# A graph layer and an attention layer on one core: weights reloaded into a third buffer, a store behind a write, and row maxima moved forward

## The chip, the cores and the metric

The kernel runs on one core of one Trainium2 chip. The metric is the device time of one execution in microseconds (us). Engines: TensorE (PE, with its weight loads PEld), VectorE (DVE), ScalarE (ACT), GpSimd (POOL), and SyncE (SP), which issues every DMA of this kernel from one queue.

## What is computed

128 graphs of 128 nodes with 512 features, float32. Layer 0 is a graph convolution, layer 1 attention with 8 heads of 64; both take a layer norm with a relu, and both are added to x. The reference, cut:

```python
h = jnp.maximum(_layernorm(x, axis=-1), 0.0)
norm_adj = adj * deg_inv_sqrt[:, None] * deg_inv_sqrt[None, :]
x = x + jnp.einsum('nm,bmo->bno', norm_adj, jnp.einsum('bni,io->bno', h, weight)) + bias
h = jnp.maximum(_layernorm(x, axis=-1), 0.0)
q, k, v = (h @ Wq + bq), (h @ Wk + bk), (h @ Wv + bv)          # split into 8 heads
scores = jnp.einsum('bqhd,bkhd->bhqk', q, k) / jnp.sqrt(64)
scores = scores + (1.0 - adj)[None, None, :, :] * -1000000000.0
out = jnp.einsum('bhqk,bkhd->bqhd', jax.nn.softmax(scores, axis=-1), v)
x = x + out @ Wo + bo
```

## The kernel before

**Groups and blocks.** The batch is cut into 32 groups of 4 elements, a group into two halves of 2. The loop over t (line 1252) runs up to five blocks per round: W (graph layer's weight product for group t + 1), Q, K and V (projections of group t) and Y (attention's output product of group t - 1). Scores of group t and attention of group t - 1 stand at V0. Each block is one product of 512 x 512 x 512 by the 2 x 2 scheme of Strassen and Winograd with seven products, and inside it by a second such level; a block has seven steps, 0 to 6. Combinations of operands are additions on POOL (line 94 and lines 411 to 414), and the sums out of PSUM are additions on DVE (L478 and L493).

**PSUM.** Six banks have names: a0, a1, d0, d1, b, c. Bank c holds the seventh product, in three pieces (PHASES, line 70): piece 0 in step 6 of its own block, pieces 1 and 2 put off into steps 1 and 2 of the next block through the list `tail` (lines 557, 567, 575 and 624). Piece 2 adds to a quarter that the reads of piece 1 take, so it follows those reads. In block Y these are pieces of v's product: `bank_c<-w,op_h` on TensorE, `v<-v,bank_c` on DVE.

**The order of the work.** Nothing is scheduled by a planner: the order is written by hand. `at(t, place, f, ...)` puts a call into a plan; the place names a block, a step and a part ("V3b" is block V, step 3, ahead of the step's second part; c comes after it). `block` (line 1150) issues what is planned for a place, then that part of the step. Engines run their own instructions in the order of issue, and tiles carry the waits between engines.

**Softmax.** Scores are written to `att` (L872 on DVE with the mask for elements 0, 1 and 2; for element 3 ACT copies, L869, and POOL adds the mask later, `add_mask`, L880, planned at V4). `row_max` (L884) takes the maxima on DVE, ACT the exponentials (L896), POOL the scaling (L907). Then `flip_att` (L914) transposes 32 x 32 blocks on DVE and writes them to DRAM (L915, named `turned<-att`), and `turn_att` (L786, `att<-turned`, four DMAs) reads them back turned. `attend` (L940) multiplies by v in the order 2, 3, 0, 1.

**Weights.** Two of three buffers `w_buf` alternate between q, k, v and o; the third holds the graph layer's weights. A buffer is reloaded by `reload_w` (line 1116, DMA at L1127) in five parts of 8 slots, 512 KB each, at places that `reloads_of` gives; a reload waits until TensorE has read the old weights there. In t = 1 the weights with all their combinations are written once to DRAM by `keep_w` (L211); o's stand until then in the buffer op_o, which attention fills at V0.

**DMA.** SP's queue is one: an issue that waits (a turn for its write, a reload for a buffer) holds all behind it. `store_half` (L958) writes 512 KB of output.

Of the kernel before, what the change touches and what calls it, by code (L numbers as in the profile page):

```python
# [8 lines left out]
F32 = mybir.dt.float32  # L9
# [39 lines left out]
SLOTS = 40  # L49


PARTS = ((0, 8), (8, 16), (16, 24), (24, 32), (32, 40))
# [45 lines left out]
def kernel(  # L98
# [18 lines left out]
    P = 128  # L117
# [4 lines left out]
    NG = B // GB  # L122
# [4 lines left out]
    dp = ctx.enter_context(tc.tile_pool(name="dp", bufs=1, space=bass.MemoryType.DRAM))  # L127
# [54 lines left out]
    w_sb, w_dram = {}, {}  # L182

    w_buf = [wp.tile([P, SLOTS, P], F32, tag=f"w{i}", name=f"w{i}") for i in range(3)]
# [21 lines left out]
            nc.sync.dma_start(w_sb[name].blocks(k), blocks_in_dram(w)[row, column])  # L206

    def keep_w(name, parts=(slice(0, SLOTS),)):
        w_dram[name] = dp.tile([P, SLOTS, P], F32, tag=f"w_{name}", name=f"wd_{name}")
        for some in parts:  # L210
            nc.sync.dma_start(w_dram[name][:, some, :], w_sb[name].slots(some))  # L211

# [638 lines left out]
    def turned_in_place(g, b):  # L851

        return g == NG - 1 or g == 0 and b >= 2
# [111 lines left out]
    def at(slot, place, f, *args):  # L965
        plan.setdefault((slot, place), []).append((f, *args))

    for t in range(-1, NG + 1):


        last = t == NG - 1
        if 0 <= t - 1 < NG - 1:
            g = t - 1

            for first, final, place, f, *args in (
                ("W4", "-Y6c", "W1c" if t == 2 else "-Y6c", flip_att, 0),
                ("W6", "W4", "W4" if t == 2 else "W3", turn_att, 0),
                ("Q4c", "W0b", "Q0b", flip_att, 1),
                ("Q6", "Q0c", "Q2b", turn_att, 1),
                ("W6", "-Y3", "-Y3", exponentials, 2, 0, H // 2),  # L980
                ("Q3c", "-Y4", "-Y4", exponentials, 2, H // 2, H),
                ("Q4c", "-Y5b", "W0c" if t == 2 else "-Y5b", softmax_end, 2),
                ("K0c", "-Y5", "-Y5", exponentials, 3, 0, H // 2),
                ("K1c", "-Y6", "-Y6", exponentials, 3, H // 2, H),
                ("K3c", "W0", "W2", softmax_end, 3),
                ("K1", "W5", "Q2c", flip_att, 2),
                ("K3", "Q3", "Q6", turn_att, 2),
                ("K3", "Q1c", "Q4b", flip_att, 3),
                ("K5", "Q4b", "K0", turn_att, 3),
            ):  # L990
                place = first if t == 1 else final if last else place
                if f in (flip_att, turn_att) and turned_in_place(g, args[0]):
                    continue
                at(t - place.startswith("-"), place.strip("-"), f, g, *args)
            if t == 1:
                at(1, "K4", transpose_att, g, 2)
                at(1, "K6", transpose_att, g, 3)
            for b in (2, 3, 0, 1):
                at(t, "V0", attend, g, b)
# [15 lines left out]
        elif 1 <= t + 1 < NG and t >= 0:  # L1015
            g = t + 1
# [19 lines left out]
            at(t + 1, "Q4", attention_residual, g, 1)  # L1036
        if 1 < t <= NG:

            at(t, "Y3" if t == NG else "Q3" if last else "W3", store_half, t - 2, 1)
        if 3 <= t + 2 < NG:  # L1040
            place = (t - 1, "Y6b") if t > 1 else (t, "W0")
            at(*place, load_x, t + 2, (0,), t > 1)
# [1 line left out]
        if 2 <= t + 2 < NG:  # L1044
            g = t + 2
            if t > 0:
                at(t, "Q0b", ln1, g, 0, (0,), ())
                at(t, "Q1c", ln1, g, 0, (1,), (0, 1))
                at(t, "Q3c", ln1, g, 1)
            places = (("Q3b", "Q5b"), ("Q3b", "Q6"), ("Q5b", "K1"), ("Q6", "K2"))  # L1050
            if t == 1:
                places = (("Q4", "K0"), ("Q4", "K1"), ("K0b", "K2"), ("K1b", "K3"))
            for b, (norm, mix) in enumerate(places):
                at(t, norm, gcn_norm, g, b)
                at(t, mix, gcn_mix, g, b)
            at(t, "K2" if t > 1 else "K4" if t > 0 else "V1b", gcn_operands, g)
            at(t, "Q6" if t > 1 else "Y1" if t > 0 else "K3", gcn_residual, g, 0)
            at(t, "K1" if t > 1 else "Y2" if t > 0 else "K3", gcn_residual, g, 1)
        if 0 <= t < NG:
            g = t  # L1060
            for b in (0, 1, 3, 2):
                at(t, "V0", scores, g, b)
            if t > 0:
                at(t, "V0c", output_operands, t - 1)
            at(t, "V1b", row_max, g, 0)
            at(t, "V3b", exponentials, g, 0, 0, H // 2)
            at(t, "V4b", exponentials, g, 0, H // 2, H)
            at(t, "V6", softmax_end, g, 0)
            if last:
                at(t, "V5b", row_max, g, 1)  # L1070
                at(t, "V5b", exponentials, g, 1, 0, H // 2)
                at(t, "V6", exponentials, g, 1, H // 2, H)
                at(t, "Y1b", softmax_end, g, 1)
                at(t, "Y2", transpose_att, g, 0)
                at(t, "Y4", transpose_att, g, 1)
            else:
                if t > 0:
                    at(t, "V3b", row_max, g, 1)
                    at(t, "Y1", exponentials, g, 1, 0, H // 2)
                    at(t, "Y2", exponentials, g, 1, H // 2, H)  # L1080
                    at(t, "Y4", softmax_end, g, 1)
                else:
                    at(t, "V4b", row_max, g, 1)
                    at(t + 1, "W2", exponentials, g, 1, 0, H // 2)
                    at(t + 1, "W3", exponentials, g, 1, H // 2, H)
                    at(t + 1, "Q3b", softmax_end, g, 1)
                at(t, "V6b", row_max, g, 2)
                at(*((t, "V4") if t > 1 else (1, "Y1") if t > 0 else (1, "Q3")), add_mask, g, 3)
                at(*((t, "Y3c") if t > 1 else (1, "Y3b") if t > 0 else (1, "Q5b")), row_max, g, 3)
        if last:  # L1090
            g = t
            at(t, "Y0", row_max, g, 2)
# [18 lines left out]
    uses, reading = [], [-1]  # L1111
# [4 lines left out]
    def reload_w(n, part):  # L1116
        if n >= len(uses):
            return
        name = uses[n]
        if name == "o last":  # L1120
            if part == len(PARTS) - 1:
                load_w(name, wo, w_buf[n % 2])
            return
        if part == 0:
            w_sb[name] = Weight(w_buf[n % 2])
        some = slice(*PARTS[part])
        nc.sync.dma_start(w_sb[name].t[:, some, :], w_dram[name][:, some, :])  # L1127

    def reloads_of(t):

        when = {
            "Q": ((t, "Q5" if t > 1 else "K1"), (t, "K1"), (t, "K1"), (t, "K1"), (t, "K3")),
            "K": ((t, "K5"), (t, "V0c"), (t, "V0c"), (t, "V0c"), (t, "V0c")),
            "V": ((t, "V3"), (t, "Y0"), (t, "Y0"), (t, "Y0"), (t, "Y3")),
            "Y": ((t, "Y4"), (t + 1, "W2"), (t + 1, "W4"), (t + 1, "Q1"), (t + 1, "Q1")),
        }
        if t + 1 == NG - 1:

            when["Y"] = ((t, "Y4"), (t + 1, "W2"), (t + 1, "W2"), (t + 1, "Q0"), (t + 1, "Q2c"))
        if t == 1:  # L1140

            when["K"] = ((1, "V0c"),) * len(PARTS)
        for kind in "QKVY":
            if kind in "QKV" and t == NG:
                continue
            reading[0] += 1
            for part, place in enumerate(when[kind]):
                at(*place, reload_w, reading[0] + 2, part)
# [10 lines left out]
    def prologue():  # L1159
# [70 lines left out]
        at(1, "Q2c", combine_inner, "k", nc.gpsimd, (6, 7, 8))  # L1230
        at(1, "Q3c", combine_w, "o", nc.gpsimd)
        at(1, "Q5", combine_inner, "o", nc.gpsimd)
        at(1, "K3", keep_w, "o", (slice(0, 16), slice(16, SLOTS)))
        at(1, "Q6", keep_w, "k")
        at(1, "W0c", output_bias)
        at(1, "K6c", attention_residual, 0, 0)
# [2 lines left out]
    with tc.manual_schedule(  # L1239
        engines={  # L1240
            mybir.EngineType.PE,
            mybir.EngineType.DVE,
            mybir.EngineType.Activation,
            mybir.EngineType.Pool,
            mybir.EngineType.SP,
        }
    ):
        prologue()
        for t in range(1, NG + 1):
            reloads_of(t)  # L1250

        for t in range(NG + 1):
            if t > 0:
                block(t, "W", t + 1, gcn_weight)
            if t < NG:
                block(t, "Q", t, lambda g: qk(g, 0))
                block(t, "K", t, lambda g: qk(g, 1))
                block(t, "V", t, values)
            block(t, "Y", t - 1, attention_out)
            if 0 < t < NG:  # L1260
                store_half(t - 1, 0)
            elif t == NG:
                store_half(t - 1, 1, slice(0, 256))
# [41 lines left out]
```

## Time and profile before

| what | value |
|---|---|
| median of 3 runs | 2254.13 us (2252.61 to 2254.39) |
| the profiled execution | 2246.82 us |
| its span, first to last instruction | 2245.0 us |
| PE, DVE, ACT, POOL busy | 2204.6, 1882.2, 1294.1, 1869.6 us |
| DMA | 599.24 MB, 90.8% of 16 engines' span |
| mean granted TensorE clock | 0.998 |

Rows of a timeline read: start us, duration us, engine, line, operation, tiles written and read, shapes, how many were merged, and in brackets the idle time before them with what ended it. Rows of waits read: who waited, for whom, sum in us, times, longest. Lines such as L142 or L94 belong to helpers, so groups are told apart by their tiles. Several rows of one engine overlap a little, because the pipeline of an engine takes the next instruction before the last has ended.

### The profile page before, as it was taken

The page shows a single profiled execution, that of the slowest core. Times are in us where ns is not written, and L with a number is a line of the kernel's source. Part 1 is how long each engine was busy: PE and PEld are TensorE (multiplying, and loading weights), DVE is VectorE, ACT ScalarE, POOL GpSimd, SP SyncE. Part 2 cuts the span into 40 slices and gives each one's busy share as a digit, 9 for nine tenths or more (in the row PEclk, how much of TensorE's full clock was granted, in tenths as well). Part 3 has the DMA queues.
Part 4 walks back from the last instruction along what each step waited for, and adds up shares of the span by engine and source line. Part 5 has one row for each costly group of instructions (what it writes and reads, how often), then busy time and mean ns, then how long its engine had stood idle before and what let it go on. Part 6 is the DMA issues. An engine that isn't in the chain of part 4 may idle for free.

```text
span 2245.0 us, 78807 instructions
## 1 busy us (share of the span) xinstructions
PE 2204.6 (98%) x31597; PEld 1879.9 (84%) x31597; DVE 1882.2 (84%) x4252; ACT 1294.1 (58%) x3813; POOL 1869.6 (83%) x1994
## 2 busy tenths in 40 slices
PE   9989999999999999999999999999999999999989
PEld 7778888888888888888888888888888888888877
DVE  7778888888888888888888888888888888888876
ACT  3566655656556656557566566565565565575434
POOL 6897988888888988888988888888889888889744
PEclk9999999999999999999999999999999999999999
DMA  5389999999999999999999999999999999999974
GB/s 162 142 257 286 261 294 281 259 299 261 287 291 282 257 287 262 289 285 267 287 270 283 290 282 266 298 261 289 284 277 264 286 269 302 274 270 286 265 214 154
DMA packets 908109, 599.24 MB, mean 267 GB/s; under 512 B 765664, under 2 KB 772960, under 8 KB 907104
## 3 DMA queue, kind: packets, MB, share of 16 engines
q1 hardware_dynamic: 907744, 594.20, 90.8%
q8 instruction: 250, 4.10, 0.8%
q14 instruction: 115, 0.94, 0.1%
HBM read 455.68 MB, written 138.41 MB: 265 GB/s over the span
## 4 chain that ended last, share of the span: by engine, by line
PE 63%; DVE 17%; DMA 4%; SPq 3%; issue 2%; ACT 0%; DVEq 0%; ACTq 0%
PE bank_a L142 23%; PE bank_d L142 14%; DVE xt L478 8%; PE bank_b L142 7%; PE bank_c L142 7%; DVE xt L493 3%; SPq L786 3%; PE pa L142 3%; PE bank_d L865 3%; DVE att L914 3%; PE po L940 2%; DMA turned<-att 2%; DMA att<-turned 2%; DVE q L478 1%; PE bank_b L940 1%
## 5 line engine op out<-in xcount | busy, mean ns | idle before, releaser
L896 ACT ACTIVATE att<-att,nmx 128x128 f32<-128x128 f32 x1024 | 408.8, 510 | 49.0 <-DVE nmx L884 47.1
L907 POOL TENSOR_TENSOR att<-att,rsm 128x1024 f32<-128x1024 f32 x121 | 229.7, 1899 | 174.6 <-PE bank_d L142 100.6
L142 PE MATMUL bank_a<-op_h,w 128*64 128x256 f32 x2976 | 352.8, 379 | 0.0
L808 ACT ACTIVATE q<-bank_a,bqk 128x256 f32<-128x256 f32 x192 | 80.1, 468 | 397.3 <-PE bank_a L142 397.3
L478 DVE TENSOR_TENSOR xt<-xt,bank_d 128x512 f32<-128x512 f32 x610 | 271.6, 471 | 11.7 <-PE bank_d L142 0.8
L142 PEld LDWEIGHTS bank_a<-op_h,w 128*64 128x64 f32 x2976 | 207.2, 137 | 81.8 <-issue 0.2
L94 POOL TENSOR_TENSOR op_o<-op_o 128x256 f32<-128x256 f32 x297 | 211.8, 737 | 15.1 <-DVE v L478 3.3
L142 PE MATMUL bank_d<-op_h,w 128*64 128x128 f32 (+1 forms) x3424 | 221.6, 275 | 0.0
L896 ACT ACTIVATION_READ_ACCUMULATOR att<-att,nmx 128x1 f32 x1024 | 212.4, 207 | 0.0
L94 POOL TENSOR_TENSOR op_a<-op_a 128x256 f32<-128x256 f32 x279 | 198.2, 735 | 15.1 <-ACT v L822 5.4
L142 PEld LDWEIGHTS bank_d<-op_h,w 128*64 128x64 f32 x3424 | 195.1, 137 | 6.7 <-issue 0.2
L94 POOL TENSOR_TENSOR op_h<-op_h 128x256 f32<-128x256 f32 x270 | 191.3, 731 | 9.4
L371 ACT ACTIVATE h<-xt,nb,rs 128x512 f32<-128x512 f32 x142 | 174.3, 1233 | 17.9 <-POOL nb L356 16.2
L142 PE MATMUL bank_a<-w,op_o 128*64 128x256 f32 x1536 | 182.2, 379 | 0.0
L142 PE MATMUL bank_a<-w,op_h 128*64 128x256 f32 x1488 | 177.9, 381 | 0.0
L142 PE MATMUL bank_a<-w,op_a 128*64 128x256 f32 x1488 | 176.5, 379 | 0.0
L493 DVE TENSOR_TENSOR xt<-bank_a,xt 128x512 f32<-128x512 f32 x252 | 166.1, 680 | 2.8 <-PE bank_a L142 2.8
L822 ACT COPY v<-bank_a 128x512 f32<-128x512 f32 x96 | 56.4, 587 | 181.1 <-PE bank_a L142 144.8
L884 DVE TENSOR_REDUCE nmx<-att 128x8 f32<-128x1024 f32 x128 | 155.0, 1211 | 0.1
L914 DVE STREAM_TRANSPOSE att<-att 128x1024 f32<-128x1024 f32 x122 | 153.1, 1255 | 0.3 <-ACT att L896 0.2
L376 POOL TENSOR_TENSOR xt<-xt,b_o 128x1024 f32<-128x1024 f32 x62 | 147.4, 2379 | 0.0
L142 PEld LDWEIGHTS bank_a<-w,op_o 128*64 128x64 f32 x1536 | 107.2, 137 | 41.8 <-issue 0.3
(198 smaller groups left out, 5843.2 us busy)
## 6 DMA issues: line engine op xcount, KB each, us to landing
w<-wd_v SPq DMA_DIRECT2D x155, 512.0 KB, 6.2
w<-wd_o SPq DMA_DIRECT2D x155, 512.0 KB, 9.8
w<-wd_q SPq DMA_DIRECT2D x150, 512.0 KB, 5.3
w<-wd_k SPq DMA_DIRECT2D x150, 512.0 KB, 6.9
turned<-att SPq DMA_DIRECT2D x122, 512.0 KB, 4.8
att<-turned SPq DMA_DIRECT2D x488, 128.0 KB, 3.9
out_dram<-xt SPq DMA_DIRECT2D x62, 512.0 KB, 4.9
op_h<-turned_h SPq DMA_DIRECT2D x232, 128.0 KB, 4.9
```

Of the source, the lines that this page charges most:

```text
L94: engine.tensor_tensor(twice(out), twice(x), twice(y), ALU.subtract if minus else ALU.add)
L142: nc.tensor.matmul(out[y : y + P // 2], lhsT[:, y : y + P // 2], rhs, **flags)
L371: nc.scalar.activation(dst, src, AF.Relu, bias=nb[:, j : j + 1], scale=rs[:, j : j + 1])
L376: engine.tensor_tensor(t, src, bias.unsqueeze(1).to_broadcast([P, t.shape[1], D]), ALU.add)
L478: nc.vector.tensor_tensor(dst, dst, src, f)
L493: nc.vector.tensor_tensor(t, src.rearrange("p (r f) -> p r f", r=2), t, ALU.add)
L786: nc.sync.dma_start(dst[:, :, y * 32 : (y + 1) * 32], rows[y])
L808: nc.scalar.activation(dst[:, r], src[:, r], AF.Identity, bias=bqk[:, i, oc : oc + 1], scale=1.0)
L884: nc.vector.tensor_reduce(nmx, att_of(g, b), AX.X, ALU.max, negate=True)
L896: nc.scalar.activation(dst, src, AF.Exp, bias=nmx[:, h : h + 1], scale=1.0, accum_out=sm[:, h : h + 1])
L907: engine.tensor_tensor(att, att, rsm.unsqueeze(2).to_broadcast([P, H, P]), ALU.mult)
L914: nc.vector.transpose(dst, weights_of(g, b).rearrange(order, i=4))
```

## The change

- Row maxima, from t = 2 on and not in the last group: element 1 from V3b to V1b, element 2 from V6b to V3b, element 3 from Y3c to Y0c.
- Stores and DMAs: the store of the second half goes from W3 to Q0c, so that in SP's queue it stands behind element 1's write; the first part of v's weights goes from Q5 to Q2.
- The last group: k's weights go into the graph layer's buffer, all at V2 of the round before; the transposes and turns of t = 31 move; both stores go to K1.
- t = 1: statistics of the layer norm and one row maximum move back by some steps; o's weights are written in two calls, the first ahead of the reload of v.

```diff
 def keep_w(name, parts=...):
-        w_dram[name] = dp.tile([P, SLOTS, P], F32, tag=f"w_{name}", name=f"wd_{name}")
+        if name not in w_dram:
+            w_dram[name] = dp.tile([P, SLOTS, P], F32, tag=f"w_{name}", name=f"wd_{name}")
...
-                ("W6", "W4", "W4" if t == 2 else "W3", turn_att, 0),
-                ("Q4c", "W0b", "Q0b", flip_att, 1),
-                ("Q6", "Q0c", "Q2b", turn_att, 1),
+                ("W6", "Q2", "W4" if t == 2 else "W3", turn_att, 0),
+                ("Q4c", "Q1c", "Q0b", flip_att, 1),
+                ("Q6", "Q3", "Q2b", turn_att, 1),
...
-                ("K1", "W5", "Q2c", flip_att, 2),
-                ("K3", "Q3", "Q6", turn_att, 2),
-                ("K3", "Q1c", "Q4b", flip_att, 3),
-                ("K5", "Q4b", "K0", turn_att, 3),
+                ("K1", "Q2c", "Q2c", flip_att, 2),
+                ("K3", "Q4", "Q6", turn_att, 2),
+                ("K3", "Q3c", "Q4b", flip_att, 3),
+                ("K5", "Q5", "K0", turn_att, 3),
...
-            at(t, "Y3" if t == NG else "Q3" if last else "W3", store_half, t - 2, 1)
+            at(t, "Y3" if t == NG else "K1" if last else "Q0c", store_half, t - 2, 1)
...
-                at(t, "Q3c", ln1, g, 1)
+                at(t, "Q4c" if t == 1 else "Q3c", ln1, g, 1)
...
-                    at(t, "V3b", row_max, g, 1)
+                    at(t, "V1b" if t > 1 else "V3b", row_max, g, 1)
...
-                at(t, "V6b", row_max, g, 2)
+                at(t, "V3b" if t > 1 else "V6b", row_max, g, 2)
...
-                at(*((t, "Y3c") if t > 1 else (1, "Y3b") if t > 0 else (1, "Q5b")), row_max, g, 3)
+                at(*((t, "Y0c") if t > 1 else (1, "Y3b") if t > 0 else (1, "K0")), row_max, g, 3)
...
-            w_sb[name] = Weight(w_buf[n % 2])
+            w_sb[name] = Weight(w_buf[2 if name == "k" and "k" not in uses[n + 1 :] else n % 2])
...
-            "Q": ((t, "Q5" if t > 1 else "K1"), (t, "K1"), (t, "K1"), (t, "K1"), (t, "K3")),
+            "Q": ((t, "Q2"), (t, "K1"), (t, "K1"), (t, "K1"), (t, "K3")),
...
-            when["Y"] = ((t, "Y4"), (t + 1, "W2"), (t + 1, "W2"), (t + 1, "Q0"), (t + 1, "Q2c"))
+            when["Y"] = ((t, "V2"),) * len(PARTS)
         if t == 1:
+            when["Q"] = ((1, "K4"),) * len(PARTS)
...
-        at(1, "K3", keep_w, "o", (slice(0, 16), slice(16, SLOTS)))
+        at(1, "K3", keep_w, "o", (slice(0, 16),))
+        at(1, "K5", keep_w, "o", (slice(16, SLOTS),))
...
-            if 0 < t < NG:
+            if t == NG - 2:
+                at(t + 1, "K1", store_half, t - 1, 0)
+            elif 0 < t < NG:
                 store_half(t - 1, 0)
```

The columns of the table of transposes and turns are: place in t = 1, place in the last group, place in all others. Nothing is added to or taken from the arithmetic; what each engine runs stays the same in number.

## The prediction, made before the change was run

> **What bounds the kernel now.** I read the page first, then TensorE's waits, then one steady group on three engines.
>
> ```profile
> PE 2204.6 (98%) x31597; PEld 1879.9 (84%) x31597; DVE 1882.2 (84%) x4252; ACT 1294.1 (58%) x3813; POOL 1869.6 (83%) x1994
> ```
>
> TensorE is busy 98% of 2245.0 us. There is little to win, and whatever holds TensorE up is paid in full. Its list of waits, longest first (sum, times, longest):
>
> ```profile
> PE po L940 <- DMA att<-turned: 10.7, 10, 1.8
> PE bank_c L142 <- DMA w<-wd_k: 6.5, 1, 6.5
> PE bank_b L865 <- ACT op_o L406: 3.4, 1, 3.4
> PE bank_c L142 <- DVE xt L478: 2.6, 2, 2.2
> PE bank_c L142 <- DVE q L478: 2.1, 1, 2.1
> PE bank_c L142 <- DVE v L478: 1.6, 1, 1.6
> ```
>
> Each line answers to an edit. A group without a wait takes 67.79 us from its first attention product to the next one's (1921.87 to 1989.66). Everything below is measured against that group, t = 27, and "at 22.6" means 22.6 us after its first attention product.
>
> **Part 1, row maxima: a new wait.** The maxima of element 1 go from V3b to V1b, of element 2 from V6b to V3b, of element 3 from Y3c to Y0c, each 1.21 us, the next DVE row 1.13 later. V1b is free: DVE then idles 1.98 us before its next read (the row at 1933.73). Element 2 in V3b takes the place that element 1 leaves. Element 3 is different: its scores get their mask from POOL (L880), and DVE may not reduce them earlier. The DVE timeline around it:
>
> ```profile
> 1941.22 1.21 DVE L884 TENSOR_REDUCE nmx<-att 128x8 f32<-128x1024 f32 x1
> 1942.35 0.68 DVE L493 TENSOR_TENSOR xt<-bank_a,xt 128x512 f32<-128x512 f32 x1
> 1943.18 0.88 DVE L478 TENSOR_TENSOR v<-v,bank_c 128x256 f32<-128x256 f32 x2 [0.15 <-PE bank_c L142]
> ...
> 1947.43 1.21 DVE L884 TENSOR_REDUCE nmx<-att 128x8 f32<-128x1024 f32 x1
> ```
>
> POOL in the same stretch:
>
> ```profile
> 1934.90 6.62 POOL L94 TENSOR_TENSOR op_o<-op_o 128x256 f32<-128x256 f32 x9
> 1941.48 2.41 POOL L880 TENSOR_TENSOR att<-att,msk 128x1024 f32<-128x1024 f32 x1
> ```
>
> And TensorE:
>
> ```profile
> 1942.53 0.61 PE L142 MATMUL bank_c<-w,op_h 128*64 128x128 f32 x8
> ...
> 1943.62 1.04 PE L142 MATMUL bank_b<-w,op_o 128*64 128x128 f32 x16
> 1944.49 0.39 PE L142 MATMUL bank_c<-w,op_h 128*64 128x128 f32 x4
> ```
>
> The first maximum shown (element 2) disappears from its place, so the xt read starts when its product ends, 1939.93 + 1.90 = 1941.83, and ends near 1942.5. Next in DVE's queue now stands element 3's maximum. The mask ends at 1941.48 + 2.41 = 1943.89, so DVE stands still for 1.4 us. Behind it are queued the two reads of v's bank_c, and then xt's reads of bank_d and bank_b: maximum at 1943.93, reads at 1945.06, done at 1945.94 instead of 1944.06. TensorE's last four products of that bank write a quarter that these reads take, so they can't start before. They started at 1944.49; they will start at 1945.98, 1.49 later, and TensorE, with one queue, stands. With 0.05 for the slower first matmul after a wait: **1.54 us**. DVE makes up its own delay, since the maximum is gone from Y3c, so nothing further down waits.
>
> Is the mask late in every group? POOL has no idle time from 14.29 before the first attention product (where ACT's statistics release it) to the mask; its order is unchanged, and what releases it keeps its distance to TensorE. In 23 of the groups t = 3 to 29 the mask ends 22.0 to 22.1 after the first attention product; DVE arrives at 20.7. So 27 x 1.54 = **+41.6**. In t = 3, 5, 17 and 24 it ended 0.7, 1.5, 0.4 and 0.6 later, after a DMA or DVE held POOL; I take half of these 3.2: **+1.6**. In t = 30 it ends at 18.80: +0.2. In t = 2 POOL has two more additions (attention_residual, 2.38 each) and the mask ends at 239.39: maximum and reads give 241.48, against 236.33 before: +5.15, less a 0.30 wait at 247.79 that the removed maximum caused.
>
> That wait is long enough for the clock. The granted clock fell to 0.66 in 145 to 150 after the 3.40 wait, to 0.52 in 2180 to 2187 after the 6.51 one, and stayed 1.00 after those of 2.25 and 1.76. So 1.54 costs only itself, and 5.15 costs about half of a 3.4 us stretch: +1.7. t = 2: **+6.6**.
>
> [...]
>
> Bounds of the wait per group: 0, if the mask were ready at 20.7; above, the row that shows this mechanism at t = 1, where a 2.51 us addition stands ahead of the same two reads:
>
> ```profile
> 166.78 0.44 PE L142 MATMUL bank_c<-w,op_h 128*64 128x128 f32 x4 [1.64 <-DVE v L478]
> ```
>
> I take 1.54, nearest to that row and to the queue's own arithmetic.
>
> **Part 2, the store behind the write, v's first part ahead of the turn.** The waits at L940 are for element 3's turned weights. In the group at 625:
>
> ```profile
> 607.67 1.16 DVE att L914
> ...
> 611.67 3.75 DMA turned<-att
> ...
> 622.53 3.63 DMA att<-turned
> ```
>
> Element 3 was transposed by 608.82, but its write went out at 612.3: SP is one queue, and stood at element 1's turn, whose write (600.06) landed at 607.6 behind a 512 KB store (597.64). Now the store follows that write, and v's first 512 KB go out before SP reaches that turn, not between writes and turns of elements 2 and 3. The store is worth 1.3 us of the queue (512 KB at the 403 GB/s of 125 to 130), v's issue on SP 0.4 to 0.8. With 1.7 to 2.1 us less, against waits of 0.3 to 1.8, all go: 10.7 less t = 2's 0.8 (there POOL sets the end), and 0.19 that each costs beyond itself (418.99 to 488.75 is 69.76, a wait of 1.76): **-11.6**. Bounds: 0 and -11.6. v's part waits for q's reads in Q1, over before that turn can go; behind it stands only the turn.
>
> **Part 3, last group (t = 31).** k's weights go to the graph layer's buffer, at V2 of t = 30, so its wait goes, 6.51. With it goes the half clock: from 2182.08 to the first attention product 7.28 us, clean 5.04 (1984.62 to 1989.66), 2.24. The 2.25 wait at 2161.41 goes too: three transposes (1.24 each) stood ahead of bank_c's reads, now one. Next late is element 3's turn: SP, relieved of k and both stores, lands it near 2178, and TensorE arrives at 2178.4. **-11.0**; bounds -8 and -11.
>
> **Part 4, t = 1.** The 3.40 wait is for o's weights leaving the buffer that op_o needs: their first write (issued 132.26) landed at 143.0 behind four parts of v (2 MB). Now v follows it. First attention product to first v product is 13.15 us there, 7.37 clean: -5.8 with the clock. Moving statistics and a maximum in Q (1.6 and 1.13 of DVE) shortens the waits of 1.0 and 2.1: -1.3. Next late: element 3's mask ends at 167.57, its maximum ran at 169.95; 7 us earlier it waits: I give back 3.1. **-4.0**; bounds 0 and -7.1. o's second write now goes behind v, before POOL's 148.32 needs it.
>
> **Sum.** 41.6 + 1.6 + 0.2 + 6.6 - 11.6 - 11.0 - 4.0 = +23.4. The profiled execution took 2246.82, so 2270.2; the median shown, 2254.13, is 7.3 above it, and the difference is carried over: **2277.5 us**.
>
> **Rivals.** *Faster:* the mask is ready in time, or the reads are not in TensorE's way. Only the gains remain, 11.6 + 11.0 + 4.0 + 0.8 = 27.4: 2226.7. Against it: POOL's row above, without idle time before it. It decides from a wait of 0.7 per group down ((26.6 - 8.4) / 27), that is a mask 0.8 earlier. Chance 0.12; in between, within 0.2% of no change (4.5 us, what a measurement of this kernel can tell), 0.04. *The new order of DMAs doesn't do what it says:* DMA queues are full (90.8%), and the writes land as late as before: +11.6, 2289.1. For it: landings of 7.5 us. Against: in t = 27 the write left 15.2 us before the first attention product, 2.6 to 3.1 earlier than in waiting groups, and the turn landed 1.9 before it. Chance 0.14. The forecast has 0.70: its own range, with t = 1 and t = 31 at their bounds (+7, -3.1) and 3 either way for the waits, is 2271 to 2288. The range reaches past the second rival, and down by the 7 that executions differ: 2264 to 2291; outside is the faster case. Faster 0.12, same 0.04, slower 0.84.
>
> **What would show it.** Right: a new line in TensorE's waits, bank_c L142 for DVE v, about 27 times 1.4; on DVE an idle time before the fourth maximum, released by POOL's mask; groups of 69.3 us; no po line, no wd_k line, no half clock near 145 and 2180. Wrong: groups of 67.8 with the maximum ending before TensorE's bank_c, or po waits still there.

## The result and the profile after

The changed kernel takes **2270.28 us** (median of 6 runs, 2267.28 to 2280.41), the kernel before 2254.26 beside it (6 runs, 2248.81 to 2263.36): ratio 1.0075, 95% interval 1.0047 to 1.0102. It is 16 us slower; 2277.5 (2264 to 2291) was predicted. The profiled execution took 2267.28 us, its span is 2265.5, 20.4 more than before (2265.46 and 2245.04). Of the page, the engines and the row of the DMA queue (packets, MB, share of 16 engines):

```profile
PE 2206.0 (97%) x31597; PEld 1883.5 (83%) x31597; DVE 1885.9 (83%) x4252; ACT 1285.8 (57%) x3813; POOL 1867.9 (82%) x1994
...
q1 hardware_dynamic: 907744, 594.20, 90.6%
```

TensorE works as long as before, 2206.0 us to 2204.6; nearly all that is lost is waiting. Its list of waits (us in sum, times, longest; lines behind the edit are one higher than before):

```profile
PE bank_c L142 <- DVE v L479: 31.4, 27, 2.9
PE po L941 <- DMA att<-turned: 11.8, 12, 2.8
PE pa L142 <- ACT h L372: 5.7, 5, 3.7
```

The wait that Part 1 foretold is there: 25 of the 27 times stand in the groups t = 3 to 29 (26.7 us), the others in t = 1 (1.80, before 1.64) and t = 2 (2.88). The wait for wd_k (6.5) and that for op_o (3.4) are gone. But the wait for the turned weights (po) is not: 11.8 after 10.7. And the third line has grown from 1.6 to 5.7.

One group (t = 21, first attention product at 1530.11) on DVE, with start, duration and in brackets the idle time before a row:

```profile
1550.11 0.69 DVE L494 TENSOR_TENSOR xt<-bank_a,xt 128x512 f32<-128x512 f32 x1 [0.57 <-PE bank_a L142]
1552.13 1.22 DVE L885 TENSOR_REDUCE nmx<-att 128x8 f32<-128x1024 f32 x1 [1.32 <-DMA w<-wd_q]
1553.26 0.87 DVE L479 TENSOR_TENSOR v<-v,bank_c 128x256 f32<-128x256 f32 x2
```

POOL in that stretch:

```profile
1543.10 6.62 POOL L94 TENSOR_TENSOR op_o<-op_o 128x256 f32<-128x256 f32 x9
1549.69 2.40 POOL L881 TENSOR_TENSOR att<-att,msk 128x1024 f32<-128x1024 f32 x1
```

And TensorE:

```profile
1551.86 1.04 PE L142 MATMUL bank_b<-w,op_o 128*64 128x128 f32 x16
1554.19 0.44 PE L142 MATMUL bank_c<-w,op_h 128*64 128x128 f32 x4 [1.28 <-DVE v L479]
```

Read it from the mask down. The mask ends at 1552.09, the maximum starts at 1552.13 (the DMA in its bracket is not what releases it; the mask's end is 0.04 away), the two reads behind it start at 1553.26, and TensorE's last piece of v starts at 24.08 after the first attention product, where the group of before had 22.62.

First attention products of the rounds cut the span into stretches; the last column is the sum of the prediction's terms in that stretch:

| stretch | before, us | after, us | difference | predicted |
|---|---|---|---|---|
| start to t = 2 | 212.67 | 212.78 | +0.1 | -4.0 |
| t = 2 | 68.99 | 74.38 | +5.4 | +6.6 |
| t = 3 to 29 | 1843.42 | 1863.30 | +19.9 | +31.6 |
| t = 30 to the end | 119.95 | 115.00 | -5.0 | -10.8 |

### The profile page after: what moved, and what is told of

Same layout as the page of the kernel before. It is cut to its first block, busy times and chain, and to the rows that moved or that the text cites. A ratio compares the mean times of both kernels' runs of the same rounds, so it can differ in the third digit from the quotient of the medians.

```text
span 2265.5 us, 78742 instructions
## 1 busy us (share of the span) xinstructions
PE 2206.0 (97%) x31597; PEld 1883.5 (83%) x31597; DVE 1885.9 (83%) x4252; ACT 1285.8 (57%) x3813; POOL 1867.9 (82%) x1994
## 5 line engine op out<-in xcount | busy, mean ns | idle before, releaser
L897 ACT ACTIVATE att<-att,nmx 128x128 f32<-128x128 f32 x1024 | 402.8, 504 | 0.6 <-DVE nmx L885 0.6
```

What stands on the lines that cost most here:

```text
L897: nc.scalar.activation(dst, src, AF.Exp, bias=nmx[:, h : h + 1], scale=1.0, accum_out=sm[:, h : h + 1])
```

## The experiments

Twelve kernels in three sets (1 to 4, 5 to 8, 9 to 12), each set on one chip beside its own runs of the kernel before. "Clean" is the time of a steady group without a wait for turned weights, "mean" that of the 27 groups t = 3 to 29, "po" the sum of TensorE's waits for turned weights; these three are from the profiled execution of each, which can lie up to 10 us from the median. The ratios are those on record and are not the quotients of the medians beside them.

| kernel | median us (runs) | ratio to before, 95% interval | clean | mean | po |
|---|---|---|---|---|---|
| before | 2254.26 (6) | 1 | 67.79 | 68.27 | 10.7 |
| after | 2270.28 (6) | 1.0075, 1.0047 to 1.0102 | 68.92 | 69.01 | 11.8 |
| 1: after, third maximum back | 2260.28 (10) | 1.0016, 0.9998 to 1.0035 | 67.79 | 68.77 | 21.9 |
| 2: before, third maximum alone | 2270.59 (4) | 1.0062, 1.0038 to 1.0087 | 68.93 | 69.00 | 6.7 |
| 3: after, third maximum behind the reads | 2260.74 (10) | 1.0030, 1.0006 to 1.0054 | 68.09 | 68.88 | 20.6 |
| 4: after, mask first | 2260.77 (10) | 1.0024, 1.0004 to 1.0043 | 67.51 | 68.79 | 27.7 |
| 5: after, statistics back | 2269.33 (6) | 1.0061, 1.0039 to 1.0083 | 68.92 | 69.19 | 17.9 |
| 6: as 1, v's part back | 2249.51 (12) | 0.9978, 0.9961 to 0.9996 | 67.79 | 68.75 | 24.0 |
| 7: as 1, store back | 2254.22 (12) | 0.9989, 0.9969 to 1.0009 | 67.79 | 68.53 | 20.9 |
| 8: four edits on after | 2248.67 (12) | 0.9972, 0.9954 to 0.9991 | 67.51 | 68.61 | 27.1 |
| 9: as 8, less read | 2231.16 (5) | 0.9870, 0.9844 to 0.9897 | 67.51 | 68.10 | 13.5 |
| 10: before, less read | 2238.71 (6) | 0.9911, 0.9889 to 0.9934 | 67.79 | 67.93 | 3.4 |
| 11: after, less read | 2266.97 (12) | 1.0038, 1.0022 to 1.0055 | 68.97 | 69.04 | 7.6 |
| 12: as 8, store back | 2253.06 (12) | 0.9969, 0.9949 to 0.9989 | 67.51 | 68.46 | 22.4 |

The kernel before stood at 2253.88 beside 1 to 4, at 2256.20 beside 5 to 8 and at 2258.63 beside 9 to 12; across sets the ratios are to be compared.

### 1 to 4: is it the mask's wait?

Theory: the maximum of element 3 waits for POOL's mask and holds up the reads that TensorE needs. Rival: the loss is in the new order of DMAs, or in the maxima of elements 1 and 2.

1, the changed kernel with this maximum back in its old place:

```diff
-                at(*((t, "Y0c") if t > 1 else (1, "Y3b") if t > 0 else (1, "K0")), row_max, g, 3)
+                at(*((t, "Y3c") if t > 1 else (1, "Y3b") if t > 0 else (1, "K0")), row_max, g, 3)
```

> The changed kernel with element 3's row maximum alone put back to Y3c from t = 2 on. Theory (DVE waits there for POOL's mask, and v's reads of bank c and then TensorE stand behind it): the 27 waits of bank_c for DVE v go, groups fall from 68.92 to 67.8 us, 27 x 1.13 = 30.5 and about 5 in t = 2 are won: some 2236 us where the changed kernel has 2270 and the kernel before 2254, so 0.8% below the kernel before. Rival (the moved DMAs or the other maxima lengthen the groups): it stays near 2270, 0.7% above the kernel before.

2, the kernel before with the opposite edit and nothing else (Y3c to Y0c).

> The kernel before with element 3's row maximum alone put forward to Y0c from t = 2 on. Theory: 18 groups without a wait for turned weights get 1.13 us longer each (20), those with such a wait hardly (their wait covers the mask's), t = 2 some 5: about 2280 us, 1.1% above the kernel before. Rival (only the new order of DMAs together with it costs): no change, 2254.

3, the changed kernel with the maximum at Y1c, behind those reads.

> The changed kernel with element 3's row maximum at Y1c, behind v's reads of bank c and one read of xt, still ahead of its old place. Theory: the mask has ended by then (22.0 us after the first attention product, DVE gets there near 22.9), DVE does not stand, the bank_c waits go: 2236 us as with the maximum back in Y3c, or up to 10 less, if the small wait in W at bank_c (0.36 a group) stays away too. Rival (any maximum this early delays the reads that TensorE needs): between 2236 and 2270.

4, the changed kernel with the mask ahead of POOL's nine additions:

```diff
-                at(*((t, "V4") if t > 1 else (1, "Y1") if t > 0 else (1, "Q3")), add_mask, g, 3)
+                at(*((t, "V0b") if t > 1 else (1, "Y1") if t > 0 else (1, "Q3")), add_mask, g, 3)
```

> The changed kernel with the maximum left at Y0c, and POOL's mask of element 3 moved ahead of the 13 additions for the attention's output operands (V0b). Theory (it is the mask that is late): the maximum runs at once, 20.7 to 21.8, the reads end near 22.7, TensorE waits 0.1 instead of 1.5 a group: 2236 to 2245 us. The additions end 2.4 later; if TensorE needs them sooner a wait of bank_b or bank_d for POOL's op_o appears in Y. Rival (the maximum's own 1.13 us on DVE is the cost, whoever releases it): hardly below 2270.

Kernel 2 settles the mechanism. This one line, put into the kernel before, brings the wait and a loss as large as that of the whole change, within the intervals (1.0062 and 1.0075). About 2280 us was expected and 2270.59 came: in its profile the waits for turned weights fell from 10.7 to 6.7 us while the new one came. Of its waits:

```profile
PE bank_c L142 <- DVE v L478: 37.0, 30, 3.4
```

In 1, 3 and 4 the wait is gone and clean groups are 67.79, 68.09 and 67.51. Yet no kernel comes near the 2236 or less that the gains of the change would give; all three stand at 2260. The waits for turned weights have doubled. In kernel 1:

```profile
PE po L941 <- DMA att<-turned: 21.9, 19, 2.8
```

All three were expected between about 2226 and 2245 and missed it. So the second reason of the prediction, that the new order of DMAs removes these waits, is false. Beside that, 3 has clean groups 0.30 longer than 1 (8 us in 27 groups) and takes the same time; 4 has groups 0.28 shorter and takes the same time. Something other than the engines' work sets the pace here.

### 5: the start

```diff
-                at(t, "Q4c" if t == 1 else "Q3c", ln1, g, 1)
+                at(t, "Q3c", ln1, g, 1)
```

> The changed kernel with one edit undone: in t = 1 the statistics ln1 of the second half stand at Q3c again. Theory: in the changed kernel the layer norm's scale on POOL stands behind the combination of o (5.19 us), TensorE waits 3.66 us at 122.6 for ScalarE's h, and half clock follows from 124.9 to 131.8 (6.83 us, about 3.4 of them lost). With the statistics ahead of the combination the wait and that half clock go: the first attend of t = 2 comes 5 to 7 us earlier than 212.8 and the time falls to about 2264. Rival: POOL does the same work in the same stage, so that the combination of o and its write come 5 us later and a wait for the weights of o returns (before had 3.4 us there): 2270, no change. What is left of the change's loss (the waits for the mask, 31.4 us) stays in both.

In the changed kernel, POOL's layer norm at t = 1 stands behind the combination of o, and TensorE waits for the h that ACT makes from it. One row of POOL:

```profile
118.69 5.19 POOL L288 TENSOR_TENSOR op_o<-op_o 128x512 f32<-128x512 f32 x4
```

One of TensorE:

```profile
126.25 1.97 PE L142 MATMUL pa<-ant,h 128*64 128x128 f32 x16 [3.66 <-ACT h L372]
```

Half clock follows from 124.9 to 131.8 (the granted clock of 125 to 130 is 0.50). With the statistics back, wait and half clock are gone, as expected, and t = 1 reaches its first attention product at 137.06 instead of 141.53. The time is the same all the same: t = 2 gets there at 213.81, after 212.78. In kernel 5, TensorE shows why:

```profile
213.81 1.98 PE L941 MATMUL po<-att,v 128*64 128x128 f32 x16 [4.61 <-DMA att<-turned]
```

The 4.5 us are waited off at the next door, and half clock comes with this wait too (213.3 to 220.1; the sixteen products of this row take 1.98 us, those at 212.78 in the changed kernel 1.09). In every kernel here the first attention product of t = 2 lies between 210.7 and 213.8, however early t = 1 was. Theory and rival were both wrong about the place; "no change" was right.

### 6 to 8: is it the order around the turns?

Theory: v's 512 KB, put ahead of element 1's turn, make SP's issue of it slow, and what stands behind comes late. Rival: the store does.

6, on kernel 1:

```diff
-            "Q": ((t, "Q2"), (t, "K1"), (t, "K1"), (t, "K1"), (t, "K3")),
+            "Q": ((t, "Q5"), (t, "K1"), (t, "K1"), (t, "K1"), (t, "K3")),
```

> The changed kernel with element 3's maximum back behind the reads (Y3c) and v's first part back at Q5, behind the turn of element 1; the store of the finished group stays behind the write of element 1. Theory: it is v's 512 KB, ahead in the queue, that makes the issue of the turn's four DMAs take 8 us instead of 4, so that the turned weights land late: with it moved back the waits for the turned weights fall from 21.9 us (with v's part ahead) to below the 10.7 of the kernel before, to 0 to 6 us, since the write still goes 2 us earlier; time about 2240 to 2247. Rival: it is the store, 512 KB as well, that now stands just ahead of the turn: the waits stay at 15 to 22 us and the time at 2257 to 2260.

7, on kernel 1:

```diff
-            at(t, "Y3" if t == NG else "K1" if last else "Q0c", store_half, t - 2, 1)
+            at(t, "Y3" if t == NG else "Q3" if last else "W3", store_half, t - 2, 1)
```

> The changed kernel with element 3's maximum back at Y3c and the store of the finished group back at W3, ahead of the write of element 1; v's first part stays ahead of the turn. Theory (v's part is what delays the turn): the issue of the turn still takes 8 us, now from a write that leaves 2 us later, and the waits for the turned weights are as many or more than the 21.9 us of the kernel with the maximum alone back; 2258 to 2270. Rival (the store is what delays it): the waits fall to about 10 us, as before the change; 2245 to 2250.

8, the changed kernel with the edits of 4, 5 and 6, and the last group's transposes and turns in their old places:

```diff
-                ("W6", "Q2", "W4" if t == 2 else "W3", turn_att, 0),
-                ("Q4c", "Q1c", "Q0b", flip_att, 1),
...
+                ("W6", "W4", "W4" if t == 2 else "W3", turn_att, 0),
+                ("Q4c", "W0b", "Q0b", flip_att, 1),
...
```

> The changed kernel with four edits: the mask of element 3 at V0b, ahead of POOL's combination for the output, so that the early maximum finds it added; v's first part back at Q5; the statistics of t = 1 back at Q3c; and the flips and turns of the last group at the places they had before, with k's weights still in the third buffer. Theory: clean groups of 67.5 us (27 of them, 0.3 less than before: 8 us), few waits for the turned weights (under 6 us, against 10.7 before), 4 us less at t = 1 and 8 to 11 less in the last group: 2220 to 2235, faster than the kernel before by 0.8 to 1.5%. Rival: the waits for the turned weights stay as in the kernel with the mask moved (27.7 us), since the store alone makes them: 2245 to 2255, no different from before.

In 6 and 7 neither the theory nor the rival holds: the waits are 24.0 and 20.9 us. Putting one of the two back is worth something in the times (0.9978 and 0.9989 after 1.0016), but the profiles do not show it: in the steady groups the mean moves by 0.02 and 0.24 only. The profiled execution of 1 is 6.6 us below its median and that of 6 is 4.8 above, so these two columns can hide a gain. Kernel 8 met the numbers of its rival (27.7 us of waits, 2245 to 2255), though the reason given there, that the store alone makes the waits, does not survive kernel 12. It shares the shortest clean groups, 67.51, and waits about as much as 4:

```profile
PE po L941 <- DMA att<-turned: 27.1, 16, 3.7
```

What its groups gain in work they lose in waits. Its first attention products show a rhythm: several groups of 67.51, then two to four in which the wait grows (1.6 and 2.1; 1.0, 2.3 and 3.7), the last lengthened by the wait and, in these two cases, its half clock (71.50 and 74.29, which is 1.9 and 3.1 more than a clean group and the wait), after which the turned weights are in time again. That looks like a queue that falls behind when it is asked to do a group in 67.5 us.

### 9 to 12: is it the load of the DMA engines?

Theory: the 16 DMA engines have no time left. The steady stretch from 420 to 2060 of the kernel before (start and end, length, then busy time and instructions of PE, PEld, DVE, ACT and POOL, granted clock, share of the DMA engines, GB/s):

```profile
420.00:2060.00 1640.00, 1627.85 (x23842) 1402.62 (x23842) 1404.68 (x3221) 972.93 (x2858) 1408.04 (x1491) 1.00 0.97 279
```

97% busy. The share of 90.8% on the page includes the ends. 9, 10 and 11 leave out 512 KB of 19.0 MB per group, the last part of o's weights, far from the turns; those slots then hold older weights, so these kernels only serve to price the load. That is 1.28 us, by the landings of four such parts one after the other in the kernel before (1933.22, 1934.48, 1935.74, 1937.05). The same edit is made to kernel 8, to before and to after:

```diff
+        if name == "o" and part == 4:
+            return
         some = slice(*PARTS[part])
```

> The kernel with the four edits, and the last 512 KB of o's weights left out of every reload from the DRAM copy (the slots keep what the buffer's previous weights left there, so the output is not the reference's): about 19.2 MB a group become 18.7, far from the turns in the order of DMAs. Theory of the full queue: the 16 DMA engines are busy 96 to 97% of the steady time and every transfer waits behind 5 to 9 us of others, so the turned weights come late whenever a group gets shorter. With 1.3 us of transfers less per group they land earlier, the waits for them fall from 27.1 us to under 8 in the profiled execution, the steady groups go from a mean of 68.61 to 67.5 to 67.8, and the time from 2248.7 to 2215 to 2226. Rival (the order around the turns makes them late, not the load): waits of 20 us and more, 2243 to 2250.

> The kernel before with the same 512 KB of o's weights left out of every reload (output not the reference's). Theory of the full queue: its waits for the turned weights, 10.7 us in the profiled execution, go to under 4, the steady groups from a mean of 68.27 to 67.8, the time to about 2236 to 2243. Rival: no change, 2254. Beside the changed kernel with the same left out it also prices the mask's wait alone: 27 groups at 1.13 to 1.54, 30 to 42 us, without the DMA queue in the sum.

> The changed kernel with the same 512 KB of o's weights left out of every reload (output not the reference's). Theory of the full queue: the groups are tied to the mask's end, 68.9 us each, whether DMAs are late or not, so little changes in them (mean 69.01 to 68.9); the late turns of the last group and of t = 2 shrink by a few us: 2257 to 2268. Rival: if the turned weights cost time in these groups beside the mask, it falls by as much as the kernel before does, 12 to 15 us, to 2255.

12 is kernel 8 with the store back at W3, so that of the new order of DMAs only the last group's is left.

> The kernel with the four edits, and the store of the finished group back at W3, ahead of the write of element 1, so that nothing of the new order of DMAs is left but the last group's. Full queue: the order moves the wait from one transfer to another and the mean of the steady groups stays at 68.3 to 68.7: 2243 to 2252, within 0.25% of the kernel with the four edits (2248.7). Rival (the store behind the write is what makes element 1's turn late): the waits fall under 12 us and the time to 2230 to 2240.

The kernel before gains 0.9%, 20 us, from 2.7% less to transfer, and its waits go from 10.7 us to these:

```profile
PE po L940 <- DMA att<-turned: 3.4, 4, 1.3
```

Its steady stretch:

```profile
420.00:2060.00 1640.00, 1634.03 (x23954) 1412.53 (x23950) 1408.91 (x3226) 971.87 (x2862) 1414.57 (x1499) 1.00 0.95 273
```

Its mean group goes to 67.93, nearly clean. Kernel 9 goes from 0.9972 to 0.9870, with its waits halved:

```profile
PE po L941 <- DMA att<-turned: 13.5, 10, 2.4
```

More than the 8 us expected, and 2231.16 us where 2215 to 2226 was: at 67.51 a group the DMAs are behind even so. 12 equals 8 (0.9969 and 0.9972): the place of the store does not matter there. So less load is shown to remove waits, and no order tried did. That the order costs nothing is not shown: with the same clean groups of 67.79 the mean is 68.27 in the kernel before and 68.77 in kernel 1, which has the whole new order. Nor do 9 to 11 tell the 16 engines from SP's one queue: the part left out is also one DMA less to issue, and SP's issuing takes 39.5 us per group in kernel 10 after 41.8 in the kernel before. The reads of turned weights land no sooner after their issue (median 4.1 us in kernel 10, 3.9 before), so what is won is that they are issued earlier.

Kernel 11 is the other half of the answer. The changed kernel hardly gains from the same relief, 1.0038 after 1.0075 by the ratios (intervals that overlap), 2266.97 after 2270.28 by the medians of two sets, and its groups stay at 69.0:

```profile
PE bank_c L142 <- DVE v L479: 34.0, 28, 5.1
PE po L941 <- DMA att<-turned: 7.6, 8, 2.6
```

So the two waits do not add up. With the load eased, the change costs 2266.97 - 2238.71 = 28.3 us, by spans 29.4. With the full load it costs 16: the kernel before pays some 20 us to the DMA load, and the changed one pays little of that, because it is standing at the mask anyway. In the changed kernel's own profile, the groups t = 10 and t = 16 start with waits of 0.99 and 0.32 for turned weights and still take 68.91 and 68.94: POOL's mask keeps its distance to work that was not late, and the wait for the mask shrinks (from 1.28 to 0.05 and 0.75). The cover has its limits: t = 17 and t = 26, with 0.67 and 0.99, take 0.3 more than a clean group, and t = 4, with 2.23 in two waits, 1.5 more.

The scatter points the same way. The runs of the kernel before spread over 18 us in that set (2249.19 to 2267.57); with less to read over 7 (2235.16 to 2242.59, 6 runs), and of the changed kernel with less to read over 6 (2264.56 to 2270.53, 12 runs). But kernel 9, with less to read too, spreads over 10 (2224.13 to 2233.99, 5 runs).

Kernels 6, 8 and 12 beat both kernels, by 0.2 to 0.3% of before. The lowest ratios are those of 8 and 12: the mask ahead of POOL's additions, the early maxima, v's part and the statistics in their old places, and of the change the last group's buffer. What holds 8 back, by kernel 9, is the DMA load.

## Why the prediction was right, and where it was wrong

The forecast, slower by a new wait at the mask, was right in its mechanism; the time came out 7 us lower, inside the range. Two of its four terms were right in kind, one stands on a false reason, one is nought. Errors of both signs cancelled: the terms are off by -11 (Part 1) to +6 us (Part 3), their sum by 3 (20.4 us of span for 23.4). The nearness of the time is in part luck.

**Part 1, "27 x 1.54 = +41.6": mechanism right, size too large.** The piece starts 1.46 later, as worked out, and the mask ends 21.92 to 22.02 after the first attention product in 23 of the 27 groups (22.11 to 23.46 in t = 3, 4, 17 and 26). But a clean group grew by 1.13 (67.79 to 68.92), 30.5 in 27. The rest is a small wait of before that the moved maximum takes away. TensorE in block W of the kernel before:

```profile
1954.91 1.04 PE L142 MATMUL bank_b<-w,op_a 128*64 128x128 f32 x16
1956.10 0.44 PE L142 MATMUL bank_c<-w,op_o 128*64 128x128 f32 x4
```

And of the changed kernel, the same two rows:

```profile
1564.66 1.04 PE L142 MATMUL bank_b<-w,op_a 128*64 128x128 f32 x16
1565.53 0.39 PE L142 MATMUL bank_c<-w,op_o 128*64 128x128 f32 x4
```

From row to row it was 1.19 and is 0.87: 0.32 comes back there, and 1.46 less 0.32 is 1.14. Such a gap is seen in the starts only, not in brackets. It goes with the place of element 3's maximum, not with the delay: it is 1.19 in every steady group of the five kernels that have the maximum at Y3c (before, 1, 6, 7 and 10) and 0.87 in the others, kernel 4 among them, where no maximum waits for the mask:

```profile
1554.00 1.04 PE L142 MATMUL bank_b<-w,op_a 128*64 128x128 f32 x16
1554.87 0.39 PE L142 MATMUL bank_c<-w,op_o 128*64 128x128 f32 x4
```

So the step that failed in this term is "nothing further down waits": it was read as no new wait, and that the maximum at Y3c had been causing one was put at nothing. The t = 2 term, +6.6, measured +5.4, with the half clock (3.4 us from 241.0) that it foresaw.

**Part 2, "1.7 to 2.1 us less, against waits of 0.3 to 1.8, all go": this step failed.** It took the late transfers for a matter of their order, although its own rival named the full queue. Turned waits went up to 21.9 us as soon as the mask's wait was out of the way (kernel 1), and no order tried removed them (6, 7, 8, 12); less load cut them from 10.7 to 3.4 (10) and halved them (9). By accident the term's size is nearly met. (Of its working, 69.76 less 67.79 less 1.76 is 0.21, not 0.19.) Steady groups went from a mean of 0.48 above clean to 0.09 above clean, 27 x 0.39 = 10.6 us, because the mask's wait covers late transfers. The sum for t = 3 to 29 is 30.5 - 10.6 = +19.9, as in the table.

**Part 3, -11.0: right only where the turned weights are in time.** The wait for wd_k is gone. From t = 30 to the end kernel 8, with the old places for the last turns, takes 110.84 us and before 119.95: -9.1. The changed kernel gets -5.0, since element 3's turn, which I put "near 2178", ahead of TensorE, lands late:

```profile
2204.53 1.09 PE L941 MATMUL po<-att,v 128*64 128x128 f32 x16 [0.55 <-DMA att<-turned]
2208.41 1.97 PE L941 MATMUL po<-att,v 128*64 128x128 f32 x16 [2.79 <-DMA att<-turned]
```

Half clock goes with it (2207.1 to 2213.9). Kernel 6 keeps the new places of these turns and takes 110.7 us, with v's first part back at Q5, where kernel 1 takes 112.7: in these two profiles the late turn goes with v's part at least as much as with the places.

**Part 4, -4.0: nothing.** The wait for op_o went, but moving the statistics behind POOL's 5.19 us made a wait of 3.66 with half clock, which the step did not look for on POOL. Kernel 5 shows that even without it the gain ends at t = 2, where the kernel before already waited 0.82 for turned weights.

**The median, "the difference is carried over".** The 7.3 us by which the median of before exceeds its profiled execution were carried over whole, and the median of the changed kernel is only 3.0 above its profiled execution: 4 us of the forecast were too much. That the changed kernel hides part of a scatter of the DMA waits would fit, but is not shown: its six runs spread over 13 us, those of before over 15. Both other rivals fell: in none of the 27 groups does the late piece start before 24.0 (22.62 when clean), and of "the writes land as late as before" only the late landings are true, not their price.

**What stays open.** Kernels 6 and 7 are faster than 1 by 0.4 and 0.3% in the times, in another set and with overlapping or nearly touching intervals, while their profiles show as many waits. How much of that is the order of DMAs, and how much the execution that was profiled, these runs do not tell. A kernel with the third maximum back and both v's part and the store in their old places was not run. Whether the 16 engines or SP's one queue is what the load fills also stays open.

## What to carry to other kernels

A share of busy time that includes the ends (90.8%) can hide a resource that is nearly full in the steady part (97%): before pricing the removal of a wait for a transfer, ask whether its order or the load makes it late, and try a kernel with less to transfer. An instruction that is moved away from a place can also take a wait with it that no bracket shows: compare the starts of the rows behind it. Two waits in one loop do not add up: ask of each what it covers, since a new one may cost less, and the removal of an old one may gain nothing, because another stands right behind it. When work is moved earlier in one engine's queue, look up what the moved instruction waits for on the other engine, and what needs the reads that are now behind it.

## What the runs showed of the hardware

**DMA.** At a share of 96 to 97% the mean steady group is 68.3 to 68.9 us in eight kernels whose clean groups range from 67.51 to 68.09; the share of kernel 10 is 0.95, with a mean of 67.93. The share is no exact part of the time: in stretches of 2 and 5 us it reads up to 1.12 in the kernel before (125 to 130) and 1.25 in kernel 8 (1155 to 1157). How much is moved per us varies: in the kernel before 418 GB/s from 1928 to 1930, where weights are read, at a share of 1.03, and 151 from 1972 to 1974, where attention weights are read back turned, at a share of 0.88. By these figures a share of 1 goes with 406 GB/s in the first stretch and with 172 in the second, so bytes per us alone do not tell how full the engines were.

**Clock.** All stretches of half clock in these fourteen profiles that begin and end within the span last 3.41 or 6.83 us, and within each profile they start whole multiples of 3.413 us apart (in the changed kernel at 124.93, 240.99 and 2207.07, 34 and 576 such lengths apart). The length of a wait alone does not tell whether one follows: a wait of 2.05 us at 896.2 in kernel 9 was followed by 3.41 us of half clock, one of 2.54 at 494.9 in kernel 2 and one of 3.43 at 238.4 there by none. Single waits of 3.65 us and more all were. In these profiles it goes, but for a narrow overlap, with how much TensorE is idle within one piece of 3.413 us. Cut each profile from 100 us on into pieces of that length in step with its stretches and add up the idle time between TensorE's rows: in the 45 pieces that half clock follows it is 1.94 to 3.41 us, in the 8699 others at full clock at most 2.03. In the kernels before and after alone it is 1.99 to 3.41 in 5 and at most 2.01 in 1247. The 2.05 us lie within one piece; of the 2.54, 0.96 lie in one and 1.58 in the next, and the 3.43 are split into 1.43 and 2.00. A second piece of half clock followed in 21 cases: in 20 of them the first had 0.84 us or more idle (0.32 in the other), and in the 24 cases without a second it had at most 0.75. The prediction's reading, that waits of its 1.54 us cost only themselves, holds: none of the 25 in the groups t = 3 to 29 of the changed kernel, 1.32 at most, was followed by any, and the 2.88 of t = 2 was.
